# A graph-attention kernel: the last graph's final two tiles get their roots from ScalarE and VectorE, and leave in one store

## The chip, the cores and the metric

The kernel runs on one core of a Trainium2 chip. A core has five engines that run side by side, each with its own instruction stream: TensorE (PE, matrix products), VectorE (DVE), ScalarE (ACT), GpSimd (POOL) and SyncE (SP, which here issues most of the data transfers). They wait for each other through semaphores. The metric is the device time of one execution in microseconds (us); lower is better.

## What is computed

The input is a batch of 16 graphs, each with 1024 nodes of 256 features, and a 0/1 adjacency matrix. Two layers follow each other. Each adds a weighted sum over neighbours to its input and normalizes every row:

```python
def _layernorm(x, axis=-1, eps=1e-5):
    m = jnp.mean(x, axis=axis, keepdims=True)
    v = jnp.var(x, axis=axis, keepdims=True)
    return (x - m) / jnp.sqrt(v + eps)
...
e = jnp.where(adj != 0, jnp.exp(-jax.nn.leaky_relu(logits, negative_slope=ALPHA)), jnp.zeros((), dtype=Hh.dtype))
rowsum = jnp.sum(e, axis=-1, keepdims=True)
rowsum = jnp.where(rowsum == 0.0, 1.0, rowsum)
h_prime = jnp.einsum('bnm,bmo->bno', e, Hh) / rowsum
return jax.nn.elu(h_prime)
...
x = _layernorm(x + _L0_gnn_ref(x, adj, L0_gnn_a0, L0_gnn_a1, L0_gnn_a2, L0_gnn_a3, L0_gnn_bias), axis=-1)
x = _layernorm(x + _L1_gnn_ref(x, adj, L1_gnn_W, L1_gnn_a), axis=-1)
```

Only the end of the second layer matters here. For a row of products `h`, the output is the layer norm of `x1 + elu(h)`, where `elu(h)` is written as `max(h, 0) + min(exp(h), 1) - 1`.

## The kernel before

A graph's 1024 rows are eight tiles of 128 rows (`t` from 0 to 7). The main function, `one_kind_pass`, assumes that the adjacency holds only zeros and ones. While it runs it collects evidence whether this is so; at its end a flag is read, and only if the flag is set a second function, `general_pass`, computes everything again. With these inputs it is skipped. The instruction stream of every engine therefore ends with the same steps: it reads the flag into a register (L652), takes a branch over the body of `general_pass` (L998), and joins the other engines in closing barriers (recorded under L1033).

The order of the instructions is written out by hand; no scheduler rearranges it. Each engine takes its instructions strictly in that order. For graph `b` the first layer's score and sum products run while the second layer of graph `b - 1` is finished. The last graph (15, called `last` in the code) has nothing after it, so its second layer stands alone at the end, in the part from L591 on. There, `done` is graph 14.

The helpers used at the end are these. `sum1` (L418) is one of the eight products that make a tile of the second layer; `acc` is its PSUM tile, with the row sum in column 256. `elu(b, t, acc)` (L427) takes the reciprocal of the row sum on VectorE (L435, L436), then ScalarE makes `h` (a Relu, L441) and `y` (an Exp, L442); for the very last tile VectorE makes `h` instead (L439). `add(b, t)` (L444) puts the parts together on VectorE (L447, L448) and takes mean and variance (`stats`, L276 and L277) into `mv1s`. `rstd` (L279) makes `1/sqrt(var + eps)` from a variance by six small GpSimd instructions: an addition (L283), a power of -0.5 (L285) and one Newton step (L288 to L291). `center` (L294) is `rstd` and two more GpSimd instructions, for `-mean * r` (L299, L300). `scale1` (L451) applies both to a tile on ScalarE (L304). `store` (L454) writes tiles to DRAM from SyncE (L456).

At the end of the last graph the products of tiles 0 to 3 run together; tiles 4 to 7 follow one by one. The loop from L612 ends each tile as it comes. GpSimd computes roots three times in and after it: for tiles 0 to 2 at `t == 4`, for tiles 3 to 5 at `t == 6`, then for tile 6 alone, and after the loop for tile 7. The normalized tiles leave in four stores: 0 to 2, 3 to 5, 6, and 7. The lines that order the end of it are:

```python
    t = NT - 1
    add(last, t)
    for q in range(3, t):
        scale1(last, q)
        if q == 5:
            store(last, 3, 3)
        elif q == 6:
            store(last, 6, 1)
    mv = mv1s[last][:, t : t + 1, :]
    r = rstd(mv, f"1_{last}_{t}")
    n_bad = nc.values_load(...)
    y = ys[last][:, t, :]
    nc.vector.tensor_scalar(y, y, mv[:, 0, 0:1], r, ALU.subtract, ALU.mult)
    store(last, t, 1)
```

The last tile is normalized by VectorE (L656), not by ScalarE. `values_load` stands before that instruction on every engine. Before the last graph, ScalarE uses Exp, Tanh, Relu, Square and plain scaling; no square root is taken on it.

Of the kernel before, what the change touches and what calls it, by code (L numbers as in the profile page):

```python
# [9 lines left out]
F32 = mybir.dt.float32  # L10
# [3 lines left out]
AF = mybir.ActivationFunctionType  # L14
ALU = mybir.AluOpType
# [3 lines left out]
P = 128  # L19
# [4 lines left out]
EPS = 1e-5  # L24
# [5 lines left out]
def one_kind_pass(  # L30
# [31 lines left out]
    nc = tc.nc  # L62
    B, N, D = x.shape
    NT = N // P
# [5 lines left out]
    const = ctx.enter_context(tc.tile_pool(name="const", bufs=1))  # L70
# [67 lines left out]
    nc.gpsimd.tensor_scalar(ident2, ident, 2.0, None, ALU.mult)  # L138
    minus1 = const.tile([P, 1], F32, tag="minus1", name="minus1")
    nc.vector.memset(minus1, -1.0)  # L140
    ones = const.tile([P, 1], F32, tag="ones", name="ones")
    nc.vector.memset(ones, 1.0)

    warm = const.tile([P, 1], F32, tag="warm", name="warm")
# [129 lines left out]
    def stats(y, mv, what):  # L274
        st = small.tile([P, nc.vector.BN_STATS_DIM], F32, tag="st", name=f"st_{what}")
        nc.vector.bn_stats(st, y)  # L276
        nc.vector.bn_aggr(mv, st)  # L277

    def rstd(mv, what):  # L279

        n_t = mv.shape[1]
        ve = small.tile([P, NT], F32, tag="ve", name=f"ve_{what}")[:, 0:n_t]
        nc.gpsimd.tensor_scalar(ve, mv[:, :, 1], EPS, None, ALU.add)  # L283
        r = small.tile([P, NT], F32, tag="r", name=f"r_{what}")[:, 0:n_t]
        nc.gpsimd.tensor_tensor(r, ve, power[:, 0:n_t], ALU.pow)  # L285

        n = small.tile([P, NT], F32, tag="n", name=f"n_{what}")[:, 0:n_t]
        nc.gpsimd.tensor_tensor(n, r, r, ALU.mult)  # L288
        nc.gpsimd.tensor_tensor(n, n, ve, ALU.mult)
        nc.gpsimd.tensor_scalar(n, n, -0.5, 1.5, ALU.mult, ALU.add)  # L290
        nc.gpsimd.tensor_tensor(r, r, n, ALU.mult)  # L291
        return r

    def center(mv, what):  # L294

        r = rstd(mv, what)
        n = mv.shape[1]
        mr = small.tile([P, NT], F32, tag="mr", name=f"mr_{what}")[:, 0:n]
        nc.gpsimd.tensor_tensor(mr, mv[:, :, 0], r, ALU.mult)  # L299
        nc.gpsimd.tensor_scalar(mr, mr, -1.0, None, ALU.mult)  # L300
        return [(r[:, t : t + 1], mr[:, t : t + 1]) for t in range(n)]

    def scale(y, r, mr):
        nc.scalar.activation(y, y, AF.Identity, bias=mr, scale=r)  # L304

    x1s, mv0s, r0s = {}, {}, {}
# [109 lines left out]
    hs, ys, mv1s, r1s = {}, {}, {}, {}  # L416

    def sum1(b, t, acc, m):  # L418
        nc.tensor.matmul(  # L419
            acc,  # L420
            lhsT=es[b][:, m, ts(t, P)],
            rhs=Hs[b][m],
            start=(m == 0),
            stop=(m == NT - 1),
        )

    def elu(b, t, acc):  # L427

        if t == 0:
            ys[b] = one.tile([P, NT, D], F32, tag="y" if b < B - 1 else "xT", name=f"y_{b}")  # L430
            mv1s[b] = small.tile([P, NT, 2], F32, tag="mv1", name=f"mv1_{b}")


        rinv = small.tile([P, 1], F32, tag="rinv", name=f"rinv_{b}_{t}")
        nc.vector.tensor_scalar(rinv, acc[:, D : D + 1], TINY, None, ALU.max)  # L435
        nc.vector.reciprocal(rinv, rinv)  # L436
        hs[b, t] = two.tile([P, D], F32, tag="h", name=f"h_{b}_{t}")
        if (b, t) == (B - 1, NT - 1):
            nc.vector.tensor_scalar(hs[b, t], acc[:, 0:D], rinv, 0.0, ALU.mult, ALU.max)  # L439
        else:  # L440
            nc.scalar.activation(hs[b, t], acc[:, 0:D], AF.Relu, scale=rinv)  # L441
        nc.scalar.activation(ys[b][:, t, :], acc[:, 0:D], AF.Exp, scale=rinv)  # L442

    def add(b, t):  # L444

        y = ys[b][:, t, :]
        nc.vector.scalar_tensor_tensor(y, y, 1.0, hs[b, t], ALU.min, ALU.add)  # L447
        nc.vector.scalar_tensor_tensor(y, y, -1.0, x1s[b][:, t, :], ALU.add, ALU.add)  # L448
        stats(y, mv1s[b][:, t, :], f"1_{b}_{t}")

    def scale1(b, t):  # L451
        scale(ys[b][:, t, :], *r1s[b][t])

    def store(b, t0, n):  # L454
        rows = out[b].rearrange("(t p) d -> p t d", p=P)
        nc.sync.dma_start(rows[:, ds(t0, n), :], ys[b][:, ds(t0, n), :])  # L456

    def acc1(b, t, pool, tag):
        return pool.tile([P, D + 1], F32, tag=tag, name=f"acc1_{b}_{t}")
# [36 lines left out]
    for b in range(1, B):  # L496
        prev, done = b - 1, b - 2
        last = b == B - 1
# [56 lines left out]
        for t in range(NT):  # L555
            acc = acc1(prev, t, ps_acc, "acc")
# [4 lines left out]
            if last and t == 7:  # L561
                weights(b, 0)
            elu(prev, t, acc)
            if last and t == 7:
                weights(b, 1)
            if t >= 1:
                add(prev, t - 1)
# [18 lines left out]
        if not last:  # L586
            add(prev, NT - 1)
            r1s[prev] = center(mv1s[prev], f"1_{prev}")


    last, done = B - 1, B - 2  # L591
    r1s[last] = []
    n_first = 4
    first = [acc1(last, t, *((ps_e, "e") if t < 3 else (ps_t, "t"))) for t in range(n_first)]
    for m in range(NT):
        if m >= 2:
            weights(last, m)
        if m == 5:
            add(done, NT - 1)
            r1s[done] = center(mv1s[done], f"1_{done}")  # L600
        for t in range(n_first):
            sum1(last, t, first[t], m)
# [9 lines left out]
    for t in range(NT):  # L612
        if t < n_first:
            acc = first[t]
        else:
            acc = acc1(last, t, ps_acc, "acc")
            for m in range(NT):
                sum1(last, t, acc, m)
        if t == 5:
            total = ps_t.tile([P, HT, P], F32, tag="t", name="total")[0:1, 0, 0:1]  # L620
            nc.tensor.matmul(total, lhsT=any_bad, rhs=ones, start=True, stop=True)
        elu(last, t, acc)
        if 1 <= t < NT - 1:
            add(last, t - 1)
        if t == 5:
            nc.vector.tensor_copy(flag, total)
        if t == 6:
            add(last, t)
        if t in (4, 6):
            r1s[last] += center(mv1s[last][:, ds(0 if t == 4 else 3, 3), :], f"1_{last}_{t}")  # L630
        if t == 6:
            r1s[last] += center(mv1s[last][:, 6:7, :], f"1_{last}_6")
        for q in range(2 * t - 6, 2 * t - 4) if 3 <= t < 7 else []:
            scale1(done, q)
            if q in (3, 7):
                store(done, q - 3, HT)
        if t == 6:
            for q in range(3):
                scale1(last, q)
            store(last, 0, 3)  # L640

    t = NT - 1
    add(last, t)
    for q in range(3, t):
        scale1(last, q)
        if q == 5:
            store(last, 3, 3)
        elif q == 6:
            store(last, 6, 1)
    mv = mv1s[last][:, t : t + 1, :]  # L650
    r = rstd(mv, f"1_{last}_{t}")
    n_bad = nc.values_load(  # L652
        flag, min_val=0, max_val=P, skip_runtime_bounds_check_because="a number of partitions"
    )
    y = ys[last][:, t, :]
    nc.vector.tensor_scalar(y, y, mv[:, 0, 0:1], r, ALU.subtract, ALU.mult)  # L656
    store(last, t, 1)
    return n_bad


# [310 lines left out]
def kernel(  # L971
    tc: tile.TileContext,
    x: bass.AP,
    adjT: bass.AP,
    a0: bass.AP,
    a1: bass.AP,
    a2: bass.AP,
    a3: bass.AP,
    bias: bass.AP,
    W: bass.AP,  # L980
    a: bass.AP,
    out: bass.AP,
):

    nc = tc.nc
    B, N = x.shape[0], x.shape[1]
    NCHK = B * CHECKS
    with tc.tile_pool(name="flag", bufs=1) as flagp:
        chk = flagp.tile([P, NCHK], F32, tag="chk", name="chk")
        fit = flagp.tile([P, B], F32, tag="fit", name="fit")
        n_bad = one_kind_pass(tc, x, adjT, a0, bias, W, a, out, chk, fit)
        with tc.If(n_bad > 0):  # L998
            general_pass(tc, x, adjT, a0, a1, a2, a3, bias, W, a, out)
# [37 lines left out]
```

## Time and profile before

| | us |
|---|---|
| median of 3 executions | 1303.8 (1302.4 to 1304.43) |
| the profiled execution, its own time | 1304.77 |
| its span, from the first to the last instruction | 1303.0 |
| outside the span (1304.77 - 1303.0) | 1.77 |

| engine | busy us | share of the span |
|---|---|---|
| PE | 1265.0 | 97% |
| DVE | 925.4 | 71% |
| ACT | 650.7 | 50% |
| POOL | 295.3 | 23% |

TensorE is busy nearly throughout, at a mean granted clock of 0.992. A line of a timeline, as shown below, gives the start in us from the beginning of the span, the duration in us, the engine, the line of the kernel, the operation, the tile written and the tiles read, the shapes, and in brackets how long the engine had been idle before it and what it then waited for. An engine's name with a `q` behind it is that engine's sequencer: register loads, branches, semaphore instructions and the issuing of transfers, which aren't counted as busy time.

### The profile page before, as it was taken

To read this page: it belongs to the slowest core of one execution; us is meant where nothing else is said; L and a number is where in the kernel's file an instruction comes from. 1 tells how busy PE (TensorE), PEld (TensorE's weight loads), DVE (VectorE), ACT (ScalarE), POOL (GpSimd) and SP (SyncE) were. 2 spreads that over 40 slices of the span, in tenths; PEclk is the share of its full clock that TensorE was granted. 3 is DMA by queue.
4 is the path that set the end of the run, shared out by engine and by line. 5 is a ranking of instruction groups with operands and counts; after the bars stand their busy time and mean duration, and the time that the engine had idled before them with its cause. 6 is when DMAs were issued, how large, how long until landed. Compare 5 with 4: busy or idle time off the path is not lost.

```text
span 1303.0 us, 17447 instructions
## 1 busy us (share of the span) xinstructions
PE 1265.0 (97%) x5445; PEld 1022.0 (78%) x5445; DVE 925.4 (71%) x2000; ACT 650.7 (50%) x1459; POOL 295.3 (23%) x606
## 2 busy tenths in 40 slices
PE   7979999999999999999999999999999999999995
PEld 5758788787877878788787887878778787887884
DVE  5665876868868586786868868587785868768664
ACT  4543544645545564545645545564545735446424
POOL 2212121321212222121221212223121221213203
PEclk9989999999999999999999999999999999999998
DMA  9386487694857948487594956948578594876211
GB/s 215 65 180 118 86 189 140 128 202 84 187 112 170 181 95 193 88 188 155 116 203 82 192 120 155 185 95 198 89 175 172 107 194 83 190 139 129 82 17 68
DMA packets 609173, 181.30 MB, mean 139 GB/s; under 512 B 486200, under 2 KB 591664, under 8 KB 609072
## 3 DMA queue, kind: packets, MB, share of 16 engines
q1 hardware_dynamic: 588480, 138.61, 49.0%
q0 software_dynamic: 20592, 41.48, 18.0%
q8 instruction: 46, 0.75, 0.2%
q14 instruction: 55, 0.45, 0.1%
HBM read 152.44 MB, written 61.14 MB: 164 GB/s over the span
## 4 chain that ended last, share of the span: by engine, by line
PE 82%; issue 5%; SPq 4%; DVE 4%; DMA 3%; POOL 1%; ACT 1%; POOLq 0%; DVEq 0%
PE acc L315 34%; PE acc L419 30%; PE pe L208 13%; PE pH L368 4%; SPq L244 3%; DMA mir<-tb 2%; DVE al L224 1%; DVE tb L240 1%; DVE tb L218 1%; ACT tb L216 1%; DVE al L255 1%; POOL r L285 1%; ACT low L217 0%; DMA x<-in_x 0%; SPq L248 0%
## 5 line engine op out<-in xcount | busy, mean ns | idle before, releaser
L315 PE MATMUL acc<-x,al 128*128 128x256 f32 x2048 | 449.3, 380 | 5.3 <-DVE al L255 5.3
L419 PE MATMUL acc<-H,e 128*128 128x257 f32 x2048 | 448.9, 380 | 0.6 <-DVE e L412 0.6
L315 PEld LDWEIGHTS acc<-x,al 128*128 128x128 f32 x2048 | 386.4, 190 | 62.8 <-DVE al L255 10.9
L419 PEld LDWEIGHTS acc<-H,e 128*128 128x128 f32 x2048 | 387.7, 190 | 58.4 <-DVE e L412 1.3
L208 PE MATMUL pe<-xa,xT 128*128 128x384 f32 (+3 forms) x768 | 267.3, 486 | 0.0
L208 PEld LDWEIGHTS pe<-xa,xT 128*128 128x128 f32 x768 | 141.5, 189 | 86.9 <-issue 46.0
L304 ACT ACTIVATE x<-x,mr,r 128x256 f32<-128x256 f32 x128 | 69.2, 592 | 231.6 <-POOL mr L300 199.9
L412 DVE SCALAR_TENSOR_TENSOR e<-p,pq,adj 128x1024 f32<-128x1024 f32 x128 | 159.8, 1270 | 20.8 <-DMA p<-p_row 17.8
L283 POOL TENSOR_SCALAR ve<-mv 128x4 f32<-128x4 f32 (+3 forms) x51 | 17.9, 350 | 676.5 <-DVE mv L277 671.2
L441 ACT ACTIVATE h<-acc,rinv 128x256 f32<-128x256 f32 x127 | 59.7, 470 | 192.7 <-DVE rinv L436 176.5
L216 ACT ACTIVATE tb<-pe 128x512 f32<-128x512 f32 (+1 forms) x192 | 94.3, 491 | 117.2 <-PE pe L208 78.5
L218 DVE TENSOR_TENSOR tb<-tb,low 128x512 f32<-128x512 f32 (+1 forms) x192 | 103.9, 546 | 60.2 <-ACT low L217 48.9
L368 PE MATMUL pH<-Wx,x1T 128*128 128x258 f32 x512 | 129.4, 387 | 8.5 <-issue 8.4
L435 DVE TENSOR_SCALAR rinv<-acc 128x1 f32<-128x1 f32 x128 | 20.1, 157 | 162.2 <-PE acc L419 162.1
L368 PEld LDWEIGHTS pH<-Wx,x1T 128*128 128x128 f32 x512 | 99.1, 194 | 45.5 <-issue 22.9
L121 ACT ACTIVATE junk<-adj,minus 128x2048 bf16<-128x2048 bf16 x64 | 127.3, 1989 | 0.0
L234 POOL TENSOR_TENSOR al<-ident,al 128x128 f32<-128x128 f32 x128 | 68.2, 533 | 241.2 <-DVE al L224 241.0
L224 DVE SCALAR_TENSOR_TENSOR al<-tb,adj 128x512 f32<-128x512 f32 (+7 forms) x132 | 97.5, 738 | 5.0
L323 DVE SCALAR_TENSOR_TENSOR x<-acc,bias_bc 128x256 f32<-128x256 f32 x128 | 54.0, 422 | 61.9 <-PE acc L315 61.9
L217 ACT ACTIVATE low<-pe 128x512 f32<-128x512 f32 (+1 forms) x192 | 93.0, 485 | 0.0
L255 DVE SCALAR_TENSOR_TENSOR al<-al,adj 128x512 f32<-128x512 f32 (+3 forms) x150 | 76.5, 534 | 1.9 <-DMA al<-mir 1.9
L240 DVE STREAM_TRANSPOSE tb<-tb 128x896 f32<-128x896 f32 (+6 forms) x105 | 74.8, 712 | 3.6
(63 smaller groups left out, 903.7 us busy)
## 6 DMA issues: line engine op xcount, KB each, us to landing
adj<-in_adjT POOLq DMA_DIRECT2D x30, 1024.0 KB, 9.2
x_rows<-x SPq DMA_DIRECT2D x32, 512.0 KB, 4.3
x1T<-x_rows SPq DMA_DIRECT2D x256, 64.0 KB, 2.5
x<-in_x SPq DMA_DIRECT2D x15, 1024.0 KB, 5.9
xT<-in_x SPq DMA_DIRECT2D x120, 128.0 KB, 3.4
out<-y SPq DMA_DIRECT2D x30, 512.0 KB, 5.3
p<-p_row POOLq DMA_DIRECT2D x15, 512.0 KB, 4.3
mir<-tb SPq DMA_DIRECT2D x60, 112.0 KB, 2.4
```

What stands on the lines that cost most here:

```text
L121: nc.scalar.activation(junk, rows, AF.Square, bias=minus1, scale=2.0, accum_out=chk[:, b * CHECKS + n : b * CHECKS + n + 1],)
L208: nc.tensor.matmul(pe[:, 0:w], lhsT=xTs[b][:, c, ts(jt, P)], rhs=xas[b][:, c, ds(jt * P + o, w)], start=(c == 0), stop=(c == ND - 1),)
L216: nc.scalar.activation(tb[:, ds(o, w)], pe[:, 0:w], AF.Tanh, scale=0.5)
L217: nc.scalar.activation(low[:, 0:w], pe[:, 0:w], AF.Tanh, scale=0.5 * SLOPE)
L218: nc.vector.tensor_tensor(tb[:, ds(o, w)], tb[:, ds(o, w)], low[:, 0:w], ALU.max)
L224: nc.vector.scalar_tensor_tensor(als[b][:, jt, c0:c1], tbs[b, jt][:, c0 - jt * P : c1 - jt * P], 1.0, adjs[b, jt // HT][:, jt % HT, c0:c1] ...
L240: nc.vector.transpose(tb, tb)
L255: nc.vector.scalar_tensor_tensor(v, v, 1.0, rows, ALU.add, ALU.mult)
L315: nc.tensor.matmul(acc, lhsT=als[b][:, jt, ts(t, P)], rhs=xs[b][:, jt, :], start=(jt == 0), stop=(jt == NT - 1),)
L368: nc.tensor.matmul(pt, lhsT=x1Ts[b][:, c, ts(t, P)], rhs=Wx[:, c, :], start=(c == 0), stop=(c == ND - 1),)
L412: nc.vector.scalar_tensor_tensor(es[b][:, m, :], p_bcs[b], pqs[b][:, m, 1:2], adjs[b, m // HT][:, m % HT, :], ALU.mult, ALU.min)
L419: nc.tensor.matmul(acc, lhsT=es[b][:, m, ts(t, P)], rhs=Hs[b][m], start=(m == 0), stop=(m == NT - 1),)
```

## The change

The change touches the end of the last graph alone, besides one constant set at the start.

- The roots of tiles 6 and 7 are no longer made by GpSimd. A new function `root` takes the variance of both tiles at once: ScalarE takes a square root, VectorE its reciprocal, and three VectorE instructions of two columns each do the Newton step. Ahead of this ScalarE takes the square root of a constant (`warm`), so that its table of functions is switched there.
- For the last tile, `-1 + x1` is added to `h` before the Exp's result is there, instead of to `y` afterwards.
- `add` of tile 5 moves ahead, to the end of the iteration `t == 5`; the roots of tiles 3 to 5 are computed there, and those of 0 to 2 as before at `t == 4`. These are GpSimd's last instructions.
- `scale1` and the store of tiles 0 to 2 move from the iteration 6 to 5, those of tiles 3 to 5 from behind the loop into iteration 6, ahead of the last tile's Exp.
- VectorE normalizes both tiles 6 and 7, behind `values_load`, and one store takes both.

```diff
+    eps = const.tile([P, 1], F32, tag="eps", name="eps")
+    nc.vector.memset(eps, EPS)
...
         if (b, t) == (B - 1, NT - 1):
-            nc.vector.tensor_scalar(hs[b, t], acc[:, 0:D], rinv, 0.0, ALU.mult, ALU.max)
+
+            h = hs[b, t]
+            nc.vector.tensor_scalar(h, acc[:, 0:D], rinv, 0.0, ALU.mult, ALU.max)
+            nc.vector.scalar_tensor_tensor(h, h, -1.0, x1s[b][:, t, :], ALU.add, ALU.add)
...
         nc.vector.scalar_tensor_tensor(y, y, 1.0, hs[b, t], ALU.min, ALU.add)
-        nc.vector.scalar_tensor_tensor(y, y, -1.0, x1s[b][:, t, :], ALU.add, ALU.add)
+        if (b, t) != (B - 1, NT - 1):
+            nc.vector.scalar_tensor_tensor(y, y, -1.0, x1s[b][:, t, :], ALU.add, ALU.add)
...
+    def root(t):
+
+
+        nc.scalar.activation(warm, ones, AF.Sqrt)
+        v = mv1s[last][:, t : t + 2, 1]
+        r = const.tile([P, 2], F32, tag="root", name="root")
+        nc.scalar.activation(r, v, AF.Sqrt, bias=eps)
+        nc.vector.reciprocal(r, r)
+
+        n = const.tile([P, 2], F32, tag="newton", name="newton")
+        nc.vector.scalar_tensor_tensor(n, v, EPS, r, ALU.add, ALU.mult)
+        nc.vector.scalar_tensor_tensor(n, n, -0.5, r, ALU.mult, ALU.mult)
+        nc.vector.scalar_tensor_tensor(r, n, 1.5, r, ALU.add, ALU.mult)
+        return r
...
         elu(last, t, acc)
-        if 1 <= t < NT - 1:
+        if 1 <= t < 6:
             add(last, t - 1)
         if t == 5:
             nc.vector.tensor_copy(flag, total)
-        if t == 6:
+        if t in (5, 6):
             add(last, t)
-        if t in (4, 6):
-            r1s[last] += center(mv1s[last][:, ds(0 if t == 4 else 3, 3), :], f"1_{last}_{t}")
-        if t == 6:
-            r1s[last] += center(mv1s[last][:, 6:7, :], f"1_{last}_6")
+        if t in (4, 5):
+            r1s[last] += center(mv1s[last][:, ds(3 * t - 12, 3), :], f"1_{last}_{t}")
...
-        if t == 6:
+        if t == 5:
             for q in range(3):
                 scale1(last, q)
             store(last, 0, 3)
-
-    t = NT - 1
-    add(last, t)
-    for q in range(3, t):
-        scale1(last, q)
-        if q == 5:
+        if t == 6:
+            for q in range(3, 6):
+                scale1(last, q)
             store(last, 3, 3)
-        elif q == 6:
-            store(last, 6, 1)
-    mv = mv1s[last][:, t : t + 1, :]
-    r = rstd(mv, f"1_{last}_{t}")
+
+    add(last, NT - 1)
+    r = root(6)
     n_bad = nc.values_load(
         flag, min_val=0, max_val=P, skip_runtime_bounds_check_because="a number of partitions"
     )
-    y = ys[last][:, t, :]
-    nc.vector.tensor_scalar(y, y, mv[:, 0, 0:1], r, ALU.subtract, ALU.mult)
-    store(last, t, 1)
+    for q in (6, 7):
+        y = ys[last][:, q, :]
+        nc.vector.tensor_scalar(
+            y, y, mv1s[last][:, q, 0:1], r[:, q - 6 : q - 5], ALU.subtract, ALU.mult
+        )
+    store(last, 6, 2)
     return n_bad
```

## The prediction

> **What bounds the kernel now.** I read the stretches of the span first, then the timeline of the end, then the sequencers' instructions in it.
>
> ```profile
> core 0: us, PE busy (x) PEld busy (x) DVE busy (x) ACT busy (x) POOL busy (x), PEclk, DMA share, GB/s
> 1255.00:1287.00 32.00, 31.36 (x143) 26.21 (x142) 25.06 (x67) 11.55 (x27) 9.21 (x19) 1.00 0.06 19
> 1287.00:1303.00 16.00, 0.00 (x0) 0.00 (x0) 2.68 (x8) 2.97 (x6) 5.03 (x20) 0.66 0.29 99
> ```
>
> TensorE bounds everything up to 1287 us; the 16 us after it hold no product and only 2 to 5 us of work on any engine. They are a chain of waits, and the change lies in it.
>
> ```profile
> 1287.43 0.48 DVE L439 TENSOR_SCALAR h<-acc,rinv 128x256 f32<-128x256 f32 x1
> ...
> 1288.01 0.47 ACT L442 ACTIVATE y<-acc,rinv 128x256 f32<-128x256 f32 x1 [0.69 <-DVE h L439]
> ...
> 1288.51 0.43 DVE L447 SCALAR_TENSOR_TENSOR y<-y,h 128x256 f32<-128x256 f32 x1 [0.60 <-ACT y L442]
> ...
> 1289.90 0.18 DVE L277 BATCH_NORM_AGGREGATE mv<-st 128x2 f32<-128x6 f32 x1
> ...
> 1291.30 0.24 POOL L300 TENSOR_SCALAR mr<-mr 128x1 f32<-128x1 f32 x1
> ...
> 1291.62 0.22 POOL L283 TENSOR_SCALAR ve<-mv 128x1 f32<-128x1 f32 x1
> ...
> 1293.63 0.41 DVE L656 TENSOR_SCALAR y<-y,mv,r 128x256 f32<-128x256 f32 x1 [3.55 <-POOL r L291]
> ```
>
> The last variance is ready at 1290.08, but POOL is busy with tile 6 until 1291.54 and returns tile 7's root at 1293.59. VectorE ends at 1294.04. That leaves 9 us. The sequencers' lines show them (the flag's load L652, the branch L998, the closing part L1033; minimum, median and maximum in ns, first and last start in us):
>
> ```profile
> L652 DVEq TENSOR_LOAD <-flag x1: 544/544/544, 1289.9 to 1289.9; - x1
> L652 POOLq TENSOR_LOAD <-flag x1: 497/497/497, 1293.4 to 1293.4; - x1
> L998 SPq EVENT_SEMAPHORE  x8: 17/17/17, 1294.9 to 1296.9; - x8
> L998 POOLq EVENT_SEMAPHORE  x5: 17/43/43, 1296.9 to 1299.5; - x5
> L998 POOLq COMPARE_BRANCH  x1: 45/45/45, 1293.9 to 1293.9; - x1
> L998 POOLq INC_SWDGE_SEM  x1: 636/636/636, 1299.6 to 1299.6; - x1
> L1033 SPq EVENT_SEMAPHORE  x14: 17/28/28, 1300.2 to 1302.9; - x14
> L1033 POOLq DRAIN  x3: 46/107/1865, 1300.3 to 1302.7; - x3
> ```
>
> SP is through with the last store at 1296.9 (it landed 2.6 us after its issue at 1294.1), then waits 3.2 us, until POOL's INC_SWDGE_SEM. POOL branched at 1293.9, executed nothing for 2.9 us, did two semaphore instructions, nothing for 2.4 us (1296.95 to 1299.35), then three more and a 1.87 us DRAIN to 1302.15. The barrier closes 0.8 us later. So POOL's exit, 9.1 us from its branch, sets the end, not the store.
>
> **What the Trainium skill says.** "Runtime: NRT & Kernel Launch", section "Instruction fetch mechanics": a taken branch outside the fetched window must fetch its target before execution goes on. The trace agrees: ACT (1292.1 to 1294.7), DVE (1293.6 to 1296.5) and POOL each show 2.5 to 2.9 us from branch to next instruction. I read POOL's second gap as the following block's fetch.
>
> "ScalarE: Activation LUTs", "What ACT_TABLE_LOAD costs": 1283 ns of load plus about 1380 ns of drain at each switch of function set; Sqrt is in another set than Exp. The only load in this trace took 1.28 us with nothing running ahead of it, and the next ACTIVATE began 0.01 us after it, so no run here shows the drain:
>
> ```profile
> 0.73 1.28 ACT L145 ACT_TABLE_LOAD   x1 [0.73 <-PEq L1025]
> 2.02 0.20 ACT L145 ACTIVATE warm<-minus 128x1 f32<-128x1 f32 x1
> ```
>
> "DMA: Bandwidth & Descriptors", "Anatomy of one DMA": the fixed cost, mostly completion, outweighs the bytes. The trace agrees: 128 KB stores took 2.2 and 2.6 us, the undisturbed 384 KB store 2.4.
>
> **The change part by part**, on the clock of the profiled execution.
>
> Tile 5's `add` moves ahead. DVE idles 1.95 us from 1281.60 to 1283.56; the four instructions took 1.54 us (1283.83 to 1285.37) and fit in, done at 1283.1. Without that gap they would delay tile 6's reciprocals by up to 1.5 us. POOL's eight instructions for tiles 3 to 5 start 0.1 later and take 3.1 to 3.4 us (its two groups of three tiles): done at 1286.4 to 1286.7. Moved past them on ACT are three scalings of tiles 0 to 2 (1282.0 to 1283.6, before Relu of tile 6 at 1284.03) and three of tiles 3 to 5. The latter now stand ahead of the last Exp: 1.58 us from 1286.4 or 1286.7, so ACT is free at 1288.0 to 1288.3. The Exp started at 1288.01: cost 0 to 0.3, taken 0.1. Queued behind it are the table switch and the root, all on the path. On SP the stores move to 1283.6 and 1288.1, where its queue is empty; cost nothing.
>
> Removed from DVE's path: L448 of tile 7, 0.46 us from start to start. Its replacement runs beside the Exp (DVE is idle 0.60 us there, it needs 0.43). Variance ready: 1290.08 - 0.46 + 0.1 = 1289.7.
>
> Table switch: Exp ends 1288.6, load 1.28, `warm` 0.20: ScalarE is ready at 1290.1, 0.4 us after the variance. Upper bound with the page's drain: 1291.5. Lower: a load wholly in advance, 1289.7, which the Exp ahead of it in order excludes. I take 1290.1, since the load shown brought no drain.
>
> Square root, 128x2 with a pointer as bias: small ACTIVATEs take 0.17 to 0.20 (L376, L377, L145); a pointer costs 0.085 (L441 470 ns against L216 385 ns for 256 elements): 0.29. Then four small DVE instructions, 0.2 us apart as L435 to L436: starts at 1290.4, 1290.6, 1290.8, 1291.0.
>
> The register load of the flag was hidden on DVE at 1289.9, behind POOL's root. Now it stands between the last Newton step and the scalings: it starts with that step and takes 0.54, so the first scaling starts at 1291.6 instead of 1291.2. Cost 0.4. Two scalings: 0.41 and, overlapping by 0.08 as other neighbours on DVE do, 0.33: end at 1292.35, against 1294.04. Gain 1.7.
>
> The store issues at 1292.4. 256 KB instead of 128: from the stores above 2.4 to 2.9, taken 2.6. Landed at 1295.0. One SP issue (0.35) and one landing less cost nothing either way, as they lay ahead of the last.
>
> POOL's exit: its register load falls at 1286.2, its branch at 1286.7. With all its present gaps (2.9, 2.4, 0.64 and DRAIN 1.87, 8.2 us) it is at the barrier at 1295.0. What is late next is SP behind the store: five semaphore instructions (0.35), a step to the closing part (0.1), twelve more to the drain (0.8, as 1300.2 to 1301.0): 1296.25. DVE branches at about 1291.7, is back at 1294.6; hidden by 1 us. Barrier 0.8: the span ends at 1297.05.
>
> Sum: 1303.0 - 1297.05 = 5.95 us, of which 1.7 are DVE's and 4.25 POOL's exit. The profiled execution took 1304.77, 1.77 outside its span and 0.97 above the median. Taken off the median: 1303.8 - 5.9 = 1297.9. No product is touched; `eps` adds one 0.06 us memset while DVE is idle at the start.
>
> **Rivals.**
>
> Drain at the switch: the page's 1.38 us come in between Exp and load, everything behind is late by that: 1299.3. For: the page. Against: the load shown.
>
> POOL's exit isn't its own: if its second gap and its DRAIN hung on the last store and not on its branch, the end would keep 6.4 us behind the landing: 1295.0 instead of 1296.6, 1302.2. For: POOL wakes at 1296.9, just as SP sees the store landed. Against: ACT and DVE show the same 2.5 to 2.9 us at other times.
>
> Another engine's exit: DVE, too, may have a second gap of 2.4 us behind its branch, as its stream is six instructions longer: it is ready at 1297.0, SP follows some 0.4 later, barrier: 1298.3 in the span, 1299.2. Against: only POOL of four engines shows one now.
>
> Slower: three new small tiles move every tile behind them in SBUF, by 96 bytes a partition in the built program, in all 16 graphs. If that made DVE or transfers slower where TensorE already waits (PE for L255: 5.3 us in 14 waits), the price would return in each graph's 78.7 us. From 0.53 us a graph on (8.5 us in all) the kernel is slower by over 0.2%: at least 1306.4. For: such waits exist. Against: sizes and operations are the same, and TensorE idles only 0.4 us in a graph (busy 78.31 of the 78.68 us from 249.79 to 328.47), so a wait must first outgrow what now hides it.
>
> **How the numbers follow.** Likeliest case 60% (its own range 1296.6 to 1299.0), drain 17%, POOL's exit not its own 10%, another engine's exit 7%, slower 6%. A measurement can tell about 0.2%, 2.6 us, from no change: faster is 60 + 17 + 7 = 84%, same 10%, slower 6%. The range reaches over drain and the other exit, with 1 us for the scatter of the runs before (1302.4 to 1304.4): 1296.4 to 1300.6.
>
> **What would show it.** Right: POOL's branch near 1286.7 and its DRAIN over before the store lands; SP without a 3.2 us wait for POOL; ACT_TABLE_LOAD right behind the last Exp and an ACTIVATE right behind it; DVE's TENSOR_LOAD between L612 and L673 of the new kernel. Wrong: 1.4 us of nothing around the table load; SP waiting for DVE or POOL behind the store; the last Exp well after 1288.3, because POOL's roots of tiles 3 to 5 came late; products of the last graph ending elsewhere than near 1287.

## The result and the profile after

| | before | after |
|---|---|---|
| median, us (22 executions each) | 1303.35 (1302.06 to 1305.75) | 1299.04 (1296.68 to 1304.21) |
| profiled execution, own time | 1304.77 | 1301.18 |
| its span | 1303.0 | 1299.1 |
| outside the span | 1.77 | 2.08 |
| last product ends | 1287.00 | 1289.10 |
| last tile's `rinv` to the end of the span | 15.94 | 10.01 |

The changed kernel is faster: 1299.04 against 1303.35 us, a ratio of 0.9971 with a 95% interval of 0.9963 to 0.9979. The gain is 4.3 us by the medians, where 5.9 were forecast. (The median of before that the prediction started from, 1303.8, was of three executions; 22 gave 1303.35.)

The last row of the table separates the end from the rest. It runs from the start of the first VectorE instruction that needs the last tile's products (the first of the two that make `rinv`, the reciprocal of its row sums) to the end. The change lies behind that point, and its gain there is 15.94 - 10.01 = 5.93 us; the sum in the prediction was 5.95. But in this execution the last product ended 2.1 us later than in the one of before, and 0.3 us more lay outside the span: 5.9 - 2.1 - 0.3 = 3.5, which is the difference of the two profiled executions (3.6) within rounding. The 5.93 us fall into two parts: from `rinv` to VectorE's last instruction it is 5.16 us instead of 7.00, and from there to the end 4.85 instead of 8.94.

The stretch behind the last product, in the changed kernel (the columns are those of the same view of before):

```profile
1289.00:1299.10 10.10, 0.10 (x1) 0.00 (x0) 3.65 (x13) 3.25 (x7) 0.00 (x0) 0.70 0.36 123
```

Ten microseconds instead of sixteen, and GpSimd has nothing left in them. The timeline of the changed kernel's end, shortened:

```profile
1288.30 0.24 POOL L302 TENSOR_SCALAR mr<-mr 128x3 f32<-128x3 f32 x1
...
1290.11 0.47 ACT L447 ACTIVATE y<-acc,rinv 128x256 f32<-128x256 f32 x1
...
1290.60 1.28 ACT L603 ACT_TABLE_LOAD   x1
...
1291.53 0.18 DVE L279 BATCH_NORM_AGGREGATE mv<-st 128x2 f32<-128x6 f32 x1
1291.89 0.20 ACT L603 ACTIVATE warm<-ones 128x1 f32<-128x1 f32 x1
1292.00 0.28 ACT L606 ACTIVATE root<-mv,eps 128x2 f32<-128x2 f32 x1
1292.31 0.17 DVE L607 RECIPROCAL root<-root 128x2 f32<-128x2 f32 x1 [0.60 <-ACT root L606]
...
1292.90 0.16 DVE L612 SCALAR_TENSOR_TENSOR root<-newton,root 128x2 f32<-128x2 f32 x1
1293.55 0.74 DVE L673 TENSOR_SCALAR y<-y,mv,root 128x256 f32<-128x256 f32 x2 [0.49 <-DVE root L612]
```

The Exp ends at 1290.58, the table load begins 0.02 us later, and `warm` and the square root stand right behind it. The variance was ready at 1291.71, 0.3 us before ScalarE was. Between the last Newton step (L612, start 1292.90) and the scalings (L673, start 1293.55) VectorE's sequencer loads the flag. The sequencers of the changed kernel, in the last 20 us (minimum, median and maximum in ns, first and last start in us):

```profile
L668 DVEq TENSOR_LOAD <-flag x1: 544/544/544, 1292.9 to 1292.9; - x1
L1017 SPq EVENT_SEMAPHORE  x8: 17/17/17, 1295.2 to 1297.5; - x8
L1017 POOLq EVENT_SEMAPHORE  x5: 17/43/43, 1292.2 to 1292.5; - x5
L1017 POOLq COMPARE_BRANCH  x1: 45/45/45, 1288.8 to 1288.8; - x1
L1052 SPq EVENT_SEMAPHORE  x14: 17/28/28, 1297.5 to 1299.1; - x14
L1052 POOLq DRAIN  x3: 46/107/1865, 1293.2 to 1298.9; - x3
```

GpSimd branches at 1288.8, wakes 3.3 us later, and now runs all five semaphore instructions in a row (1292.2 to 1292.5): the second gap, 2.4 us before, is gone. Its DRAIN is over at 1295.1, while the store lands at 1297.1. The closing wait of SP, first before, then after (the waits view: total us, count, longest):

```profile
SPq L1033 <- DMA adj<-in_adjT: 3.2, 1, 3.2
```

```profile
SPq L462 <- DVE y L673: 3.1, 1, 3.1
SPq L1017 <- SPq L1017: 2.2, 2, 1.8
...
SPq L1052 <- PEq L1052: 0.7, 2, 0.5
```

The releaser named before (a load of `adj` that was long over) can't be right; SP went on at 1300.2, when GpSimd's INC_SWDGE_SEM ended. After, SP waits for VectorE, then for the store, and then only 0.7 us in the barrier. The end is now set by the store.

### The profile page after: what moved, and what is told of

Read it like the earlier page. It is cut to its first block, busy times and chain, and to the rows that moved or that the text cites. A ratio compares the mean times of both kernels' runs of the same rounds, so it can differ in the third digit from the quotient of the medians.

```text
span 1299.1 us, 17437 instructions
## 1 busy us (share of the span) xinstructions
PE 1265.7 (97%) x5445; PEld 1023.9 (79%) x5445; DVE 926.5 (71%) x2006; ACT 651.2 (50%) x1461; POOL 291.2 (22%) x592
## 4 chain that ended last, share of the span: by engine, by line
PE 84%; DVE 4%; DMA 4%; SPq 4%; ACT 2%; issue 1%; POOL 0%; DVEq 0%; ACTq 0%; POOLq 0%
PE acc L421 33%; PE acc L317 32%; PE pe L210 13%; PE pH L370 5%; SPq L246 3%; DMA mir<-tb 2%; DVE al L226 1%; DVE tb L220 1%; DMA out<-y 1%; DVE tb L242 1%; ACT tb L218 1%; DVE al L257 1%; ACT low L219 1%; DVE e L414 0%; DMA p<-p_row 0%
## 5 line engine op out<-in xcount | busy, mean ns | idle before, releaser
L285 POOL TENSOR_SCALAR ve<-mv 128x4 f32<-128x4 f32 (+2 forms) x49 | 17.2, 350 | 674.7 <-DVE mv L279 669.5
L447 ACT ACTIVATE y<-acc,rinv 128x256 f32<-128x256 f32 x128 | 59.7, 467 | 35.8 <-DMA out<-y 35.8
```

## The experiments

All are measured beside the kernel before on the same chip. "The end" means the time from the last tile's `rinv` to the end of the span, as above: 15.94 us before, 10.01 after. None of these kernels leaves out any of the computation.

**GpSimd's exit.** The theory: its exit runs from its own branch, and its second gap depends on where its closing instructions lie in its stream. The changed kernel's GpSimd stream is 14 instructions shorter ahead of its closing part (592 against 606 in the traces, semaphore instructions and other sequencer work not counted). So I made it 8 instructions longer in the kernel before:

```diff
-    nc.gpsimd.memset(power, -0.5)
+    for k in range(9):
+        nc.gpsimd.memset(power, -0.5)
```

> The kernel before with eight more GpSimd memsets of the tile power at the start, where GpSimd idles; nothing else. If GpSimd's exit sets the end and its second gap (2.4 us, 1296.95 to 1299.35) is a fetch of the next block of instructions, eight more instructions ahead move the block's boundary out of the closing part: the gap goes, and the kernel is about 2.4 us faster although it does more. If the end hangs on the last store, or the gap is a wait on something else, the gap stays and the time is unchanged.

Measured: 1302.19 us (20 executions) against 1304.21, ratio 0.9986 (0.9979 to 0.9992); the end took 14.14 us. GpSimd's sequencer and SP's wait in this kernel:

```profile
L999 POOLq EVENT_SEMAPHORE  x5: 17/43/43, 1296.6 to 1297.0; - x5
L999 POOLq COMPARE_BRANCH  x1: 45/45/45, 1293.2 to 1293.2; - x1
L999 POOLq INC_SWDGE_SEM  x1: 636/636/636, 1297.1 to 1297.1; - x1
```

```profile
SPq L1034 <- DMA adj<-in_adjT: 0.9, 1, 0.9
```

The branch is followed by 3.4 us of nothing (2.9 before), but the five semaphore instructions now take 0.4 us together instead of 2.7. GpSimd still ends last, after the store, so the end follows its exit. Eight useless instructions more at the start make this kernel 2.0 us faster. The gap belongs to the place in the instruction stream and not to the store.

The other way round, the changed kernel with one GpSimd instruction that waits for the new root:

```diff
     r = root(6)
+    nc.gpsimd.tensor_scalar(warm, r[:, 0:1], 1.0, None, ALU.mult)
```

> The changed kernel with one small GpSimd instruction behind the root that reads it and writes the unused tile warm; GpSimd so cannot branch before the last root is there. If GpSimd's early exit brought the part of the gain that VectorE did not, GpSimd branches about 0.8 us after the last Newton step instead of 4 us before it, needs 3.3 us of fetch, 0.4 of semaphores, 0.6 and 1.9 us of DRAIN, and the end comes 1.5 to 2 us later than in the changed kernel, with SP through with the last store and waiting for GpSimd. If the last store alone sets the end, nothing changes.

Measured: 1301.94 us (12 executions) against 1304.21, ratio 0.9986 (0.9976 to 0.9996); the end took 11.44 us, 1.43 more than in the changed kernel, a little less than expected. (By its median this kernel is 3.7 us slower than the changed kernel with a pad on the same chip, 1298.26 us, told of below; what of that exceeds the 1.43 isn't seen in the end.) The sequencers:

```profile
L1018 SPq EVENT_SEMAPHORE  x8: 17/17/17, 1298.9 to 1300.8; - x8
L1018 POOLq EVENT_SEMAPHORE  x5: 17/43/43, 1300.4 to 1300.8; - x5
L1018 POOLq COMPARE_BRANCH  x1: 45/45/45, 1297.4 to 1297.4; - x1
L1053 POOLq DRAIN  x3: 46/107/1865, 1301.5 to 1304.0; - x3
```

The whole exit has moved with the branch: 3.0 us to the first semaphore instruction, then INC_SWDGE_SEM and a DRAIN that starts at 1301.5 and ends at 1303.4, 2.6 us after SP was through with the store (1300.8). There is no second gap, since the stream is only one instruction longer than that of the changed kernel. With 14 more, it is within one instruction as long as that of before:

```diff
-    nc.gpsimd.memset(power, -0.5)
+    for k in range(15):
+        nc.gpsimd.memset(power, -0.5)
```

> The run that holds GpSimd behind the last root, with fourteen more GpSimd memsets at the start, so that GpSimd's stream is as long ahead of its closing part as in the kernel before. If the second gap is a block's boundary, it is back between the second and third semaphore instruction (about 2.4 us), and the stretch from the last reciprocal of a row sum to the end is 13.7 to 13.9 us against 11.4 in the other hold. If the gap belonged to the old end, it stays 11.4.

Measured in one execution: 1303.23 us, the end 13.63, 2.19 more than without the 14. GpSimd's sequencer:

```profile
L1019 POOLq EVENT_SEMAPHORE  x5: 17/43/43, 1295.4 to 1298.0; - x5
L1019 POOLq COMPARE_BRANCH  x1: 45/45/45, 1292.4 to 1292.4; - x1
L1019 POOLq INC_SWDGE_SEM  x1: 636/636/636, 1298.1 to 1298.1; - x1
```

The five instructions span 2.6 us again (2.7 in the kernel before). The late branch and the 14 instructions together give back 3.6 of the 4.1 us that the end had gained behind VectorE. These three kernels settle the part on GpSimd: its exit hangs on its branch, and the second gap comes and goes with the length of its stream.

**The shift of the tiles in SBUF.** The slower rival. The changed kernel's transfers took a larger share of the queues than before (columns: packets, bytes in MB, share of 16 engines' span; then a group of loads with KB each and median us from issue to landing). Before, then after:

```profile
q1 hardware_dynamic: 588480, 138.61, 49.0%
...
xT<-in_x SPq DMA_DIRECT2D x120, 128.0 KB, 3.4
```

```profile
q1 hardware_dynamic: 588464, 138.61, 53.9%
...
xT<-in_x SPq DMA_DIRECT2D x120, 128.0 KB, 4.8
...
out<-y SPq DMA_DIRECT2D x1, 256.0 KB, 2.8
```

The bytes are the same and the loads of `xT` take 1.4 us longer. To see whether the shift alone does it, the kernel before got three unused tiles, which shift all tiles behind them by 96 bytes a partition:

```diff
+    for k in range(3):
+        pad = const.tile([P, 1], F32, tag=f"pad{k}", name=f"pad{k}")
+        nc.vector.memset(pad, 0.0)
     ones = const.tile(...)
```

> The kernel before with three unused tiles of one column in the constant pool, so that every tile behind them stands 96 bytes further on in each partition, as in the changed kernel; nothing else. If the shift is what made the 128-byte transfers slower (xT from 3.4 to 4.8 us to landing, queue q1 from 49.0 to 53.9% of the engines), this run shows q1 near 54% and xT near 4.8 us, its end from the last product on stays at 16.0 us, and it is 1 to 2 us slower than before, with more scatter. If those slower transfers were chance, or came from the new end, q1 stays near 49%, xT near 3.4 us, and the time within 0.5 us of before.

and the changed kernel got one more, so that its shift is 128 bytes:

```diff
+    pad = const.tile([P, 1], F32, tag="pad", name="pad")
+    nc.vector.memset(pad, 0.0)
     ones = const.tile(...)
```

> The changed kernel with one more unused tile in the constant pool, so that the tiles behind it stand 128 bytes further on than before instead of 96. If the 96 bytes cost the difference between the 5.95 us predicted and the 4.3 measured, this is 5.5 to 6.2 us faster than before, q1 near 49%, xT near 3.4 us. If they do not, it is like the changed kernel: 4.3 us faster, q1 near 54%.

Measured: the kernel before with 96 bytes took 1305.04 us (13 executions) against 1304.21, ratio 1.0011 (1.0002 to 1.0019); the changed kernel with 128 took 1298.26 (8 executions), ratio 0.9965 (0.9953 to 0.9976). Their queues, first the kernel before with 96 bytes, then the changed kernel with 128:

```profile
q1 hardware_dynamic: 588480, 138.61, 53.5%
...
xT<-in_x SPq DMA_DIRECT2D x120, 128.0 KB, 4.7
```

```profile
q1 hardware_dynamic: 588464, 138.61, 49.6%
...
xT<-in_x SPq DMA_DIRECT2D x120, 128.0 KB, 3.6
```

So the shift does slow the transfers, and nothing else in the change does. Which starts are slow? I thought of odd multiples of 32 bytes, and put two unused tiles, then one, into the kernel before (the first diff, with 2 and 1 for 3):

> The kernel before with two unused tiles in the constant pool: everything behind them moves by 64 bytes, so that tiles on a multiple of 64 bytes stay on one. If it is the start on an odd multiple of 32 bytes that slows the 128-byte packets, they stay at a mean of 12.8 to 12.9 ns, q1 at 49 to 50%, and the time is that of before. If any shift does it, the packets take 14.6 ns and q1 53.5%.

> The kernel before with one unused tile: a shift of 32 bytes. If packets of 128 bytes are fast only where the tiles start on a multiple of 128 bytes, they take 14.5 ns here too, as with 64 and 96; with 128 they took 12.8. If 32 is as good as 0, something other than the start is at work.

Measured: 64 bytes gave 1305.12 us (12 executions) against 1304.58, ratio 1.0004 (0.9996 to 1.0013), and its queue stood at 53.4%; that idea fell. 32 bytes, in one execution: 1303.63. The mean duration of the 128-byte packets, worked out from the packet records of each trace:

| kernel | shift, bytes | ns |
|---|---|---|
| before | 0 | 12.8 |
| before | 32 | 14.6 |
| before | 64 | 14.5 |
| before | 96 | 14.6 |
| changed, twice with the pad | 128 | 12.9, 12.8 |
| changed, first trace and run again | 96 | 14.7, 14.9 |

What it costs in time was to be told by the changed kernel with and without the pad, side by side (no edit for the first, the diff of the pad for the second):

> The changed kernel itself again, on one chip with the next run. If the 96-byte shift costs it time, it is 4 to 4.8 us faster than before, its packets of 128 bytes take 14.6 ns, and it scatters over 4 us or more.

> The changed kernel with the 128-byte shift again. If the shift of 96 costs time, this is 5.5 to 6.2 us faster than before, by 1 to 2 us faster than the changed kernel beside it, and scatters less. If the difference between the two was chance, both have the same median within 0.5 us.

Measured: 1298.39 us without (6 executions), 1298.16 with (6), against 1303.34; ratios 0.9969 (0.9957 to 0.9981) and 0.9965 (0.9952 to 0.9978). The two differ by 0.2 us, well inside their intervals. I had expected the pad to bring back the missing 1 to 2 us; that theory fell. Slower transfers are shown; that they cost time is shown only for the 96 bytes in the kernel before (0.1%), not for 64, and not in the changed kernel.

**What is left in the end.** The flag's register load stood between the last Newton step and the scalings. It was moved, on every engine, ahead of the last tile's `elu` (with the pad, for a shift of 128 bytes, as well):

```diff
+        if t == NT - 1:
+            n_bad = nc.values_load(flag, ...)
         elu(last, t, acc)
...
     r = root(6)
-    n_bad = nc.values_load(flag, ...)
```

> The changed kernel with the 128-byte shift and with the flag's register load moved ahead of the last tile's elu, so that VectorE does it while it waits for the last products instead of between root and scaling. If the load costs 0.4 us there, the stretch from the last tile's reciprocal of the row sum to the end is 9.5 to 9.7 us instead of 10.0, and the kernel is 6.0 to 6.6 us faster than before. If something else (the table switch, SP's landing) sets the end, the stretch stays at 10.0.

Measured: 1298.59 us (5 executions) against 1304.58, ratio 0.9954 (0.9940 to 0.9967), which doesn't set it apart from the runs with the pad alone (0.9965 both). From `rinv` to the last scaling VectorE took 4.71 us, against 5.15 and 5.16 in those two runs: 0.45 less. The end took 9.50 us, against 9.97 and 10.04. The load and the last instructions of VectorE:

```profile
L647 DVEq TENSOR_LOAD <-flag x1: 607/607/607, 1285.9 to 1285.9; - x1
```

```profile
1290.39 0.16 DVE L614 SCALAR_TENSOR_TENSOR root<-newton,root 128x2 f32<-128x2 f32 x1
1290.59 0.74 DVE L676 TENSOR_SCALAR y<-y,mv,root 128x256 f32<-128x256 f32 x2
```

From the last Newton step to the first scaling it is 0.20 us, where the changed kernel took 0.65. The load lies at 1285.9, where VectorE waits for the last products anyway.

The same kernel without the square root of a constant:

```diff
-        nc.scalar.activation(warm, ones, AF.Sqrt)
```

> The run with the early register load, without the square root of a constant ahead of the root. If that instruction is what lets the table be loaded ahead of the variance, without it the load waits for the variance, 1.1 us after the Exp's end, and the end comes about 1 us later. If the load waits for nothing anyway, it still starts right behind the Exp and the end comes 0.1 us earlier.

Measured in one execution: 1300.66 us, the end 9.62. ScalarE's timeline:

```profile
1289.96 0.47 ACT L449 ACTIVATE y<-acc,rinv 128x256 f32<-128x256 f32 x1
...
1290.45 1.28 ACT L607 ACT_TABLE_LOAD   x1
...
1291.75 0.30 ACT L607 ACTIVATE root<-mv,eps 128x2 f32<-128x2 f32 x1
```

The load still stands right behind the Exp, although its square root has to wait for the variance: the switch doesn't wait for the operands. From `rinv` to the last scaling VectorE took 4.61 us instead of 4.71, so `warm` brings nothing and costs 0.1; the end is 0.1 longer nonetheless, because the last store took 2.9 us to landing instead of 2.7. The 1300.66 comes from the body: this trace, too, has the stall told of below (1.7 us).

Last, one store for each of the two tiles instead of one for both:

```diff
         y = ys[last][:, q, :]
         nc.vector.tensor_scalar(...)
-    store(last, 6, 2)
+        store(last, q, 1)
```

> The run with the early register load, but with one store for tile 6 and one for tile 7 instead of one for both. If a landing takes longer with its size, the last one (128 KB) lands 0.2 to 0.4 us sooner after VectorE's end and the stretch from the last reciprocal to the end is 9.1 to 9.3 us. If its fixed part decides, or SP's second issue (0.35 us) eats it, it stays at 9.5 to 9.6.

Measured in one execution: 1295.94 us, the end 9.11, which is 0.39 less than with one store. The last stores, from issue to landing, with one store and with two:

```profile
out<-y SPq DMA_DIRECT2D x1, 256.0 KB, 2.7
```

```profile
out<-y SPq DMA_DIRECT2D x2, 128.0 KB, 2.3
```

The first of the two runs beside the second scaling, and the last one is half as large. This trace has the shortest end of all, 0.9 us below the change. Of that, the 0.45 of the register load are shown. The rest isn't: VectorE took 4.70 us here, as in the kernel with one store, and 0.30 of the 0.39 lie in the last landing, which varies as much without any change of size. In the run of the changed kernel itself repeated for the shift, the store of 256 KB landed just as soon after VectorE's end (2.45 us; 2.43 here), and its end took 9.67 us instead of 10.01:

```profile
out<-y SPq DMA_DIRECT2D x1, 256.0 KB, 2.4
```

Over all traces the last store took 2.4 to 2.9 us with 256 KB and 2.3 to 3.1 us with 128. That the smaller store helps stays open. So does the lead of the 1295.94: it is one execution, and its last product happened to end at 1284.8, earlier than in any other trace (1285.9 to 1292.7).

## Why the prediction was right, and what was mis-sized

The end of the profiled execution after runs 2.10 us later than that of before, so this is taken off below.

- Tile 5's `add` and GpSimd's roots: GpSimd done at 1288.54 - 2.10 = 1286.44, forecast 1286.4 to 1286.7. The last Exp began at 1288.01, not delayed at all (0.1 was taken).
- Variance ready: 1289.61, forecast 1289.7.
- Table switch: 1.28 us right behind the Exp, no drain. The drain of the Trainium skill's page "ScalarE: Activation LUTs", section "What ACT_TABLE_LOAD costs", was seen in none of the nine traces with the changed end; each has the load right behind the Exp. That rival is out.
- Square root 0.28 us (forecast 0.29), small VectorE instructions 0.2 us apart, the flag's load 0.45 us on the path (forecast 0.4; its removal gave 0.45). VectorE ended at 1294.29 - 2.10 = 1292.19, forecast 1292.35.
- The store: 2.76 us to its landing, forecast 2.6. Landed at 1297.08 - 2.10 = 1294.98, forecast 1295.0. As the same store took 2.4 us in the repeated run, a hit this close is partly luck.
- GpSimd's exit: at the barrier at 1295.10 - 2.10 = 1293.0; forecast 1295.0, with the second gap kept. The gap went, which the forecast didn't see; it changed nothing here, as SP is later either way. The rival that the exit hangs on the store is refuted by the changed kernel (the DRAIN ends 2.0 us before the landing) and by the runs that moved the branch.
- VectorE's exit: branch at 1293.61, back at 1296.60, 3.0 us, no second gap. That rival is out.
- SP's closing and the barrier: from the landing at 1297.08 to 1299.14 it is 2.06 us, forecast 2.05.

The 5.93 us in the end are thus 1.84 of VectorE (forecast 1.7) and 4.09 behind it (forecast 4.25). The time alone couldn't have told this: 1299.04 lies just outside the range given for the likeliest case (1296.6 to 1299.0), and nearer to the 1299.3 of the drain and the 1299.2 of another engine's exit than to 1297.9. It is the traces that rule these two out. And 1299.04 lies only 1.1 us from 1297.9, although the gain is 1.6 short, because the median of before that the forecast started from was 0.45 too high: that is luck.

The mis-sized term is the first one, "TensorE bounds everything up to 1287 us", carried over unchanged, with "taken off the median" behind it. The forecast took the body as fixed and the last product "near 1287"; it ended 2.1 us later here. Laid side by side product by product, TensorE after is 0.5 us behind TensorE before at 105 us, still 0.5 at 655 us, and 2.1 from 694 us to the end. All fourteen traces are like this: against the kernel before, none drifts by more than 0.03 us between 105 and 655 us or behind 694. The body scatters in its first 105 us (from 2.1 us ahead to 0.5 behind) and at one place in the middle (0 to 5.5 us). The waits of the stretch 660 to 700 us show that place, first before, then after:

```profile
ACT y L442 <- DMA out<-y: 2.4, 1, 2.4
```

```profile
ACT y L447 <- DMA out<-y: 6.8, 1, 6.8
PE acc L421 <- ACT y L447: 1.3, 1, 1.3
```

and the same stretch of the kernel whose GpSimd was held back:

```profile
ACT y L447 <- DMA out<-y: 8.6, 1, 8.6
PE acc L421 <- ACT y L447: 3.6, 1, 3.6
```

A tile's Exp has to wait until the store of an earlier `y` has left the buffer. Up to some point that is free; then no accumulator is left, and TensorE waits. The kernel before comes to 2.4 us there and loses nothing. The store waited for took 9.9 us to landing after, 5.6 before. This is in the middle of the run, in code that the change doesn't touch; TensorE falls back there by 0.5 us in the trace of the kernel before with eight GpSimd instructions more, too.

Executions over 2 us above the median of their kernel were 12 of 59 with the changed end and its variants and 3 of 94 with the kernel before; with 96 bytes of shift in the kernel before they were 3 of 13, with 64 none of 12. The shift was my explanation; the run without the pad was no slower than the one with it, and a kernel with the pad had the stall as well. So why the changed kernels meet this more often stays open.

In the gain: 4.3 us by the medians of the main measurement, 5.0 in the run repeated later (1298.39 against 1303.34), against 5.9 in the end. Of the rest, about 0.2 us are outside the span (1.8 us in the mean of the executions of before, 2.0 after). The remainder lies in the body; that it is this scatter fits the traces, but isn't shown for the executions that make the medians.

Of the slower rival, one step was right (transfers do get slower) and the price was far from enough: about 0.1% of the time (0.8 us by the medians, 1.4 by the ratio of 1.0011) in the one comparison that showed any, where 8.5 us were needed.

## What to carry to other kernels

At the end of a kernel, look at the sequencers' lines and not only at the busy time: an engine is done not with its last instruction but with its branch, its wake-up and its drain, here 6 to 8 us for GpSimd, so the engine with the longest exit should get its last work first. Take register loads off the last engine's path. A gain read from the end is right for the end; before taking it off the median, ask how far the body scatters, and compare by a mark in the trace that stands behind the body. And before putting a few tenths of a microsecond down to an edit, look at what they lie in: the landing of one and the same last store differed by 0.3 us between two traces of the same kernel.

## What the runs showed of the hardware

- Behind the taken branch GpSimd executed nothing for 2.8 to 3.4 us in all fourteen traces, and for 2.2 to 2.4 us more in five of them: the kernel before, its three versions with unused tiles (the same GpSimd stream), and the held kernel with 14 instructions more. Eight instructions more or 14 fewer removed the second gap. SP went on 0.4 us behind its own branch in every trace. The Trainium skill ("Runtime: NRT & Kernel Launch", "Instruction fetch mechanics") says that crossing a block of the instruction stream is mostly hidden. Right behind a jump it isn't, if the second gap is such a crossing. That it depends on the length of the stream is shown; that it is a fetch is my reading.
- The table load began 0.02 us behind the Exp in all nine traces with the changed end and, where no dummy call stood ahead of the root, 1.1 us before the root's variance was ready: it didn't wait for the operands of the function that needs it, so an early dummy call bought nothing.
- 128-byte packets took 12.8 to 12.9 ns where the tiles started as before or 128 bytes later, and 14.5 to 14.9 ns at 32, 64 or 96 bytes. Adding one small constant tile to the kernel before made the median load of `xT` 1.3 us longer (3.4 to 4.7), in a kernel that hides nearly all of it.
